# A graph network's second layer: its first pass in text order, and one square root for four blocks

## The chip, the core and the metric

The kernel runs on one core of one Trainium2 chip. The metric is the time of one launch on the device, in microseconds; lower is better. A core has five instruction queues: PE (matrix multiply), DVE (vector), ACT (scalar functions), POOL and SP. Each has an order of its own, and semaphores tie them together. SP only issues transfers here.

## The reference

32768 nodes with 128 features each, and 524288 edges. Two layers follow one another. The first is a graph layer with local attention and three batch norms. Its end matters here: the rows `x` plus a batch-normed `v` are layer-normed.

```python
# end of layer 0
x = _layernorm(x + _bn(h + f, g3, beta3))
# layer 1, three times
q = x @ Wq.T + bq
attn = softmax(q @ keys.T)
retrieved = attn @ values
lap = x - dinv[:, None] * segment_sum of (dinv[:, None] * x)[col] into row
x = 0.5 * x + 0.5 * (retrieved - 0.2 * lap)
# then a layer norm, the residual and a last layer norm
```

The stage under study works out the layer norm at the end of layer 0 for all rows, and the first of the three rounds of layer 1: the attention over 512 keys, and the rows scaled by `dinv`, which are spread out to the edges. Summing over the edges comes in the next stage.

## The kernel before

Nodes are handled in 64 blocks of 512 rows; a block has four chunks of 128 rows. `layer1_grid` has three stages, each with its own pools: the first pass (pool `l1p`), two passes of `for t in range(T_STEPS - 1)` (pool `l1w`), and a last one. The change is in the first pass. It and `l1w` are not under `tc.manual_schedule()`: their instructions are ordered by the framework's scheduler, which takes them from the text by priority and readiness. The last stage is. Under `tc.manual_schedule()` each engine gets its instructions in the order in which the text issues them.

A block of the first pass goes through three lists of steps; each step has a place, a number from 0 to 23.

- `first` (lines 1968 to 1990): `load` brings `v` (L1973) and `x` (L1975) in on SP. `scale` (place 7) applies the batch norm to `v` on ACT (L1978). `turn` (12) transposes it on PE (four matmuls, L1984) and adds `x` on DVE (L1985). `norm` (15) is a layer norm: four pairs of bn_stats and bn_aggr on DVE (L1080, L1081), a square root on ACT (L1083), a reciprocal (L1087) and four normalizing steps on DVE (L1089); then the rows are stored (L1989).
- `prepare` (1992 to 2017): `rows` (1) scales the rows by `dinv` (`nx`, L1998); four split steps (4, 8, 10, 14) cut them into three bf16 parts, alternating ACT (L1395, L1397) and DVE (L1396, L1393), and store them (L1394). `project` (2) transposes the rows (L2005, copy `xT` on ACT, L2007), `query` (7) multiplies by `Wq` (L2011, L2013).
- `emit` (2019 to 2070): `scores(c)` for the four chunks (0, 3, 6, 9) is a 512-column matmul (L2028), the row maximum on DVE (L1060) and the exponential on ACT with its sum (L1062). `turn(c)` (5, 8, 11, 13) transposes the probabilities (L2034) and copies them as `pt` on ACT (L2035). `retrieve` (17) sums four 512-column matmuls with `values` (L2040), copies the result as `oT` on ACT (L2043) and inverts the sums on DVE. `remain` (20) transposes it back (L2052) and makes `part_o` in two DVE steps (L2054, L2055), stored by L2056. `spread(n)` at every place from 0 to 23 is two matmuls with 384 columns (a pair, L1444) into a PSUM tile `exp`, of which there are two, and one eviction to bf16 (L1449): on ACT for even n, on DVE for odd n. Three evictions fill a tile that SP stores (L1452). `ask_pick` fetches the selection matrix of a chunk two chunks ahead (L1407).

`placed` merges the lists by place. In iteration n the loop issues `load` of block n+3, `first` of block n+2, `prepare` of n+1 and `emit` of n.

```python
return [f for _, f in sorted((x for one in lists for x in one), key=lambda x: x[0])]
```

PSUM has two tiles each of `exp`, `s` (scores, query, retrieve) and `tr` (all transposes). A pair can start only when the eviction that frees its tile is done.

Of the kernel before, what the change touches and what calls it, by code (L numbers as in the profile page):

```python
# [9 lines left out]
F32 = mybir.dt.float32  # L10
# [3 lines left out]
AF = mybir.ActivationFunctionType  # L14
OP = mybir.AluOpType
# [4 lines left out]
P = 128  # L20
D = 128
BLK = 512
NCH = BLK // P
# [885 lines left out]
def tile_gnn_resnorm(ctx: ExitStack, tc: tile.TileContext, a: dict, out: bass.AP):  # L909
# [8 lines left out]
    nc = tc.nc  # L918
    N = a["x"].shape[0]
    E = a["src"].shape[0]  # L920
    NB = N // BLK
# [38 lines left out]
    eps_c = cp.tile([P, 1], F32, name="eps_c")  # L960
# [9 lines left out]
    v = {n: vec[:, k:k + 1] for k, n in enumerate(VECS)}  # L970
# [125 lines left out]
    def layer_norm(wp, y, o, scale=None, shift=None):  # L1096
        for f in layer_norm_steps(wp, y, o, scale, shift):
            f()
# [856 lines left out]
    def layer1_grid(v_d, s3, c3):  # L1955

        exs = [Exchange("src", slots_d[t % 2], rows_d[t]) for t in range(T_STEPS)]
        with tc.tile_pool(name="l1g", bufs=1) as gp:
# [6 lines left out]
                if w < NW:  # L1965
                    picked[w] = exs[0].known_pick(wp, w)

            def first(b, st, wp, p_tr):


                def load():
                    st["v"] = wp.tile([P, BLK], F32, name="vT")
                    nc.sync.dma_start(st["v"], v_d[b])  # L1973
                    st["x0"] = wp.tile([P, NCH, D], F32, name="x1")
                    nc.sync.dma_start(st["x0"], rows_of(a["x"], b))  # L1975

                def scale():
                    nc.scalar.activation(st["v"], st["v"], AF.Identity, bias=c3, scale=s3)  # L1978

                def turn():  # L1980
                    st["x"] = wp.tile([P, NCH, D], F32, name="xn", bufs=5)
                    ps = p_tr.tile([P, NCH, P], F32, name="tr")
                    for c in range(NCH):
                        nc.tensor.transpose(ps[:, c, :], st["v"][:, c * P:(c + 1) * P], ident)  # L1984
                    nc.vector.tensor_add(st["x0"], st["x0"], ps)  # L1985

                def norm():
                    layer_norm(wp, st["x0"], st["x"])
                    nc.sync.dma_start(kept_of(xs_d[0], b), flat(st["x"]))  # L1989
                return load, [(7, scale), (12, turn), (15, norm)]  # L1990

            def prepare(t, b, st, wp, p_s, p_tr):

                ex = exs[t]

                def rows():
                    nx = wp.tile([P, NCH, D], F32, name="nx")
                    nc.vector.tensor_tensor(nx, st["x"], dinv[:, b * NCH:(b + 1) * NCH].unsqueeze(2)  # L1998
                                            .to_broadcast([P, NCH, D]), OP.mult)
                    st["r"], st["split"] = ex.split_steps(wp, b, nx, nx)  # L2000

                def project():
                    ps = p_tr.tile([P, NCH, P], F32, name="tr")
                    for c in range(NCH):
                        nc.tensor.transpose(ps[:, c, :], st["x"][:, c, :], ident)  # L2005
                    st["xT"] = wp.tile([P, BLK], F32, name="xT")
                    nc.scalar.copy(st["xT"], ps.rearrange("p c n -> p (c n)"))  # L2007

                def query():
                    ps = p_s.tile([P, BLK], F32, name="s")  # L2010
                    nc.tensor.matmul(ps, w["WqT"], st["xT"], start=True, stop=True)  # L2011
                    st["q"] = wp.tile([P, BLK], F32, name="qT")
                    nc.scalar.activation(st["q"], ps, AF.Identity, bias=v["L1_gnn_bq"])  # L2013
                return [(1, rows), (2, project), (4, lambda: st["split"][0]()), (7, query),
                        (8, lambda: st["split"][1]()), (10, lambda: st["split"][2]()),
                        (14, lambda: st["split"][3]())]

            def emit(t, b, st, wp, p_e, p_s, p_tr, share):

                ex = exs[t]  # L2020
                y = {}

                def scores(c):
                    if c == 0:
                        st["pt"] = wp.tile([P, NCH, BLK], F32, name="pt")
                        st["sums"] = wp.tile([P, NCH], F32, name="sums")
                    s = p_s.tile([P, BLK], F32, name="s")
                    nc.tensor.matmul(s, st["q"][:, c * P:(c + 1) * P], keysT, start=True, stop=True)  # L2028
                    st["pr", c] = softmax_rows(wp, s, st["sums"][:, c:c + 1])

                def turn(c):
                    ps = p_tr.tile([P, NCH, P], F32, name="tr")
                    for k in range(NCH):
                        nc.tensor.transpose(ps[:, k, :], st["pr", c][:, k * P:(k + 1) * P], ident)  # L2034
                    nc.scalar.copy(st["pt"][:, :, c * P:(c + 1) * P], ps)  # L2035

                def retrieve():
                    ps = p_s.tile([P, BLK], F32, name="s")
                    for k in range(NCH):
                        nc.tensor.matmul(ps, values[:, k, :], st["pt"][:, k, :], start=(k == 0),  # L2040
                                         stop=(k == NCH - 1))
                    st["oT"] = wp.tile([P, BLK], F32, name="oT", bufs=1)
                    nc.scalar.copy(st["oT"], ps)  # L2043
                    rec = wp.tile([P, NCH], F32, name="rec")
                    nc.vector.reciprocal(rec, st["sums"])
                    nc.vector.tensor_scalar(rec, rec, 0.5, None, op0=OP.mult)
                    st["rec"] = rec

                def remain():
                    ps = p_tr.tile([P, NCH, P], F32, name="tr")  # L2050
                    for c in range(NCH):
                        nc.tensor.transpose(ps[:, c, :], st["oT"][:, c * P:(c + 1) * P], ident)  # L2052
                    part = wp.tile([P, NCH, D], F32, name="part_o")
                    nc.vector.tensor_tensor(part, ps, st["rec"].unsqueeze(2).to_broadcast([P, NCH, D]), OP.mult)  # L2054
                    nc.vector.scalar_tensor_tensor(part, st["x"], 0.4, part, op0=OP.mult, op1=OP.add)  # L2055
                    nc.sync.dma_start(kept_of(part_d, b), flat(part))  # L2056

                def spread(n):
                    c, m = divmod(n, KS)
                    i = b * NCH + c  # L2060
                    if m == 0:
                        ask_pick(wp, i + 2)
                    ex.spread(wp, p_e, "exp", i, picked[i], st["r"][:, c, :], m, y, n % share == share - 1)
                    if m == KS - 1:
                        del picked[i]

                places = [(n, lambda n=n: spread(n)) for n in range(NCH * KS)]
                return places + [(0, lambda: scores(0)), (3, lambda: scores(1)), (5, lambda: turn(0)),
                                 (6, lambda: scores(2)), (8, lambda: turn(1)), (9, lambda: scores(3)),
                                 (11, lambda: turn(2)), (13, lambda: turn(3)), (17, retrieve), (20, remain)]  # L2070

            def placed(*lists):

                return [f for _, f in sorted((x for one in lists for x in one), key=lambda x: x[0])]
# [54 lines left out]
            def run(steps):  # L2129
                for f in steps:  # L2130
                    f()

            with tc.tile_pool(name="l1p", bufs=2) as wp, \
                    tc.tile_pool(name="l1p_exp", bufs=2, space=PSUM) as p_e, \
                    tc.tile_pool(name="l1p_s", bufs=2, space=PSUM) as p_s, \
                    tc.tile_pool(name="l1p_tr", bufs=2, space=PSUM) as p_tr:
                sts, firsts = {}, {}
                for w0 in range(2):
                    ask_pick(wp, w0)
                for n in range(-3, NB):  # L2140
                    b = n + 3
                    if b < NB:
                        sts[b] = {}
                        load, firsts[b] = first(b, sts[b], wp, p_tr)
                        load()
                    lists = []
                    if n + 2 in sts:
                        lists.append(firsts.pop(n + 2))
                    if n + 1 in sts:
                        lists.append(prepare(0, n + 1, sts[n + 1], wp, p_s, p_tr))  # L2150
                    if n >= 0:
                        lists.append(emit(0, n, sts[n], wp, p_e, p_s, p_tr, 2))
                    run(placed(*lists))
                    sts.pop(n, None)

            with tc.tile_pool(name="l1w", bufs=2) as wp, \
                    tc.tile_pool(name="l1_seg", bufs=2, space=PSUM) as p_g, \
# [3 lines left out]
                for t in range(T_STEPS - 1):  # L2161
                    sums = Sums(exs[t], wp, p_g, gc["iota1"], 2)
                    sts = {}
# [3 lines left out]
                    for n in range(-2, NB):  # L2167
                        lists = []
# [107 lines left out]
```

## Time and profile before

| | |
|---|---|
| median of three runs | 13724.5 us (13710.27 to 13725.8) |
| the profiled execution, its time | 13720.72 us |
| its span | 13718.8 us |
| PE, DVE, ACT, POOL busy over the whole span | 85%, 74%, 49%, 39% |
| first pair of the first pass starts | 6259.7 us |
| last eviction of the first pass ends | 7709.0 us |
| stage after it (`l1w`) | to about 12030 us |

How to read the lines of the profile: PE is the matmul queue, PEld its weight loads. A group names the line, the engine, the operation, what it writes and reads with the shapes, and the count; then its busy time and the mean of one instruction, and the time for which the engine stood idle just ahead of such instructions, with what ended most of it. L12 is line 12 of the kernel. A matmul of f32 operands shows as two records. In the timeline the first number is the start in the span, the second the time to the end of the row's instructions, and brackets hold the idle time before it with its releaser. A matmul's end is modelled, and one instruction's span overlaps the next one's start a little, so the time from start to start is shorter than the span.

### The profile page before, as it was taken

Reading aid. Unit: us, or ns where it says so; the run is one execution under the profiler, and the core shown is the slowest. Engines: PE = TensorE matmul, PEld = TensorE weight load, DVE = VectorE, ACT = ScalarE, POOL = GpSimd, SP = SyncE. Lnnn points to the kernel's source line nnn. Section 1 sums busy time; section 2 is a strip of 40 time slices with the busy share of each in tenths; the row PEclk is TensorE's granted clock in tenths of the full one; section 3 lists DMA queues with packets and bytes.
Section 4 is the critical chain, followed back from the end, with each engine's and each line's share of the span. In section 5 each row is a group of like instructions: output and inputs, shape, how many; then the busy total and the mean of one; then the engine's idle time right before and its main releaser. Section 6 shows DMA issues by size and latency. Waiting matters only on the chain. (4 is left out here: it accounts for less than half of the span.)

```text
span 13718.8 us, 167775 instructions
## 1 busy us (share of the span) xinstructions
PE 11728.4 (85%) x58924; PEld 5767.8 (42%) x58984; DVE 10087.5 (74%) x16572; ACT 6762.4 (49%) x10444; POOL 5314.5 (39%) x5333
## 2 busy tenths in 40 slices
PE   8988898887777888888999799999899999966666
PEld 3333333333333444444444455555455555533333
DVE  6998898879997777767888666666566666566666
ACT  4444444448884111137888566666566666600000
POOL 0000000000003777720000366666566666567777
PEclk9999999999999999999999999999999999988777
DMA  1000000007778999967888899999999999988887
GB/s 41 13 11 12 18 13 11 14 34 277 273 294 312 314 314 315 314 229 261 304 311 310 315 402 401 398 399 399 357 400 400 398 398 401 378 302 289 288 291 256
DMA packets 1339021, 3590.33 MB, mean 262 GB/s; under 512 B 197298, under 2 KB 579154, under 8 KB 1337010
## 3 DMA queue, kind: packets, MB, share of 16 engines
q1 hardware_dynamic: 968816, 2936.78, 56.6%
q0 software_dynamic: 252608, 520.41, 11.9%
q10 hardware_dynamic: 116738, 122.29, 2.6%
q8 instruction: 465, 7.62, 0.2%
q14 instruction: 394, 3.23, 0.1%
HBM read 2075.81 MB, written 1502.97 MB: 261 GB/s over the span
## 5 line engine op out<-in xcount | busy, mean ns | idle before, releaser
L1462 POOL DMA_INDIRECT listed<-rows,other x5120 | 5169.1, 1010 | 4103.9 <-issue 3140.6
L1449 ACT CAST y_o<-exp 128x768 bf16<-128x768 f32 x4352 | 3317.6, 807 | 984.7 <-PE exp L1444 732.6
L1444 PE MATMUL exp<-rows,pick 128*128 128x384 bf16 x12288 | 2818.7, 329 | 414.7 <-ACT y_o L1449 247.9
L1487 PEld LDWEIGHTS <-oh 128*128 128x128 bf16 x19456 | 1982.9, 102 | 2664.4 <-issue 1608.4
L1487 PE MATMUL seg<-y_i,oh 128*128 128x384 bf16 x12288 | 2643.7, 346 | 20.0 <-DMA y_i<-slots 18.7
L1449 DVE CAST y_o<-exp 128x768 bf16<-128x768 f32 x1792 | 1711.3, 955 | 688.9 <-PE exp L1444 576.7
L1444 PEld LDWEIGHTS <-pick 128*128 128x128 fp8e4 x12288 | 1203.3, 98 | 2054.3 <-issue 1371.6
L1487 PE MATMUL seg<-listed,oh 128*128 128x384 bf16 (+1 forms) x5120 | 1303.5, 335 | 885.5 <-DMA listed<-rows,other 848.3
L1390 POOL MEMSET rows<- 128x8 bf16 x64 | 6.8, 107 | 4022.2 <-DMA attn_d<-aT 2859.3
L1639 ACT ACTIVATE pT<-s 128x1024 f32<-128x1024 f32 x1024 | 1027.5, 1025 | 999.5 <-PE s L1614 859.7
L2103 DVE SCALAR_TENSOR_TENSOR part_i<-seg,dinv,part_i 128x128 f32<-128x128 f32 x1536 | 532.6, 347 | 1331.9 <-PE seg L1487 1320.8
L1619 DVE TENSOR_REDUCE mx<-s 128x2 f32<-128x1024 f32 x1024 | 1239.9, 1222 | 312.4 <-PE s L1614 308.4
L1614 PE MATMUL s<-k,q 32*128 32x512 f32 x4096 | 1196.7, 665 | 89.3 <-ACT pT L1639 82.0
L1635 PE MATMUL s<-ql,k 32*128 32x512 f32 x4096 | 1129.4, 646 | 63.8 <-DVE ql L1629 36.1
L1083 ACT ACTIVATE ln_rs<-ln_mv,eps_c 128x4 f32<-128x4 f32 x192 | 57.2, 298 | 1642.2 <-DVE ln_mv L1081 1641.5
L2028 PE MATMUL s<-keysT,qT 128*128 128x512 f32 x1536 | 796.0, 600 | 2.7 <-ACT pr L1062 1.7
L1432 DVE TENSOR_SCALAR_CACHE_REDUCE pick<-row_p,lane 128x512 fp8e4<-128x512 f32 x768 | 555.2, 748 | 260.2 <-PE row_p L1421 243.9
L2040 PE MATMUL s<-pt,values 128*128 128x512 f32 x1536 | 725.9, 595 | 10.7 <-ACT pt L2035 10.4
L1473 DVE TENSOR_TENSOR oh<-iota,slot 128x2432 bf16<-128x2432 bf16 x512 | 724.6, 1415 | 3.0 <-DMA slots<-y_o 3.0
L1473 DVE TENSOR_TENSOR oh<-ramp_p,slot 128x2432 bf16<-128x2432 bf16 x512 | 724.2, 1415 | 3.4 <-DMA slots<-y_o 3.4
L1487 PE MATMUL seg<-common,oh 128*128 128x384 bf16 (+1 forms) x2048 | 632.8, 351 | 69.1 <-DMA common<-rows,shared 68.6
L1421 PE MATMUL row_p<-row,ident_b 128*128 128x512 bf16 x1476 | 587.1, 398 | 95.7 <-DVE pick L1806 88.9
(404 smaller groups left out, 14138.6 us busy)
## 6 DMA issues: line engine op xcount, KB each, us to landing
slots<-y_o SPq DMA_DIRECT2D x2048, 576.0 KB
y_i<-slots SPq DMA_DIRECT2D x1024, 1152.0 KB
pick<-pick SPq DMA_DIRECT2D x1024, 192.0 KB
listed<-rows,other POOLq DMA_INDIRECT x5120
rows<-rows SPq DMA_DIRECT2D x192, 384.0 KB
part_d<-part_o SPq DMA_DIRECT2D x192, 256.0 KB
part_i<-part_d ACTq DMA_DIRECT2D x192, 256.0 KB
rows<-rows SPq DMA_DIRECT2D x64, 386.0 KB
```

What stands on the lines that cost most here:

```text
L1421: nc.tensor.matmul(ps, gc["ident"][:, w % P:w % P + 1].to_broadcast([P, P]), self.row[:, w // P, j * BLK:(j + 1) * BLK], start=True, stop= ...
L1444: nc.tensor.matmul(ps[:, j, :ROW], pick[:, o:o + P], r, start=True, stop=True)
L1449: (nc.vector.tensor_copy if to_dve else nc.scalar.copy)(dst, ps[:, :, :ROW])
L1462: nc.gpsimd.indirect_dma_start(out=g[:, k, :], out_offset=None, in_=self.table, in_offset=bass.IndirectOffsetOnAxis(ap=index[:, k:k + 1], ...
L1473: nc.vector.tensor_tensor(oh.rearrange("p c (w z) -> p c w z", z=2), ramp.rearrange("p (w z) -> p w z", z=2)[:, None].to_broadcast([P, NC2 ...
L1487: nc.tensor.matmul(ps[:, :n], oh[:, j, :], src, start=(k == 0), stop=(k == NC2 - 1))
L1614: nc.tensor.matmul(ps[:, s % 2, :], t["q", o][32 * s:32 * s + 32, c * P:(c + 1) * P], t["k", o][32 * s:32 * s + 32, :], start=True, stop=True)
L1619: nc.vector.tensor_reduce(m[:, c, 2 * i:2 * i + 2, xr[o]], st[b].pop(("two", i)), AX.X, OP.max, negate=True)
L1635: nc.tensor.matmul(ps[:, s % 2, :], t["k", o][32 * s:32 * s + 32, c * P:(c + 1) * P], t["ql", o][32 * s:32 * s + 32, :], start=True, stop= ...
L1639: nc.scalar.activation(t["p", c][:, 2 * i:2 * i + 2, :], ps, AF.Exp)
L2028: nc.tensor.matmul(s, st["q"][:, c * P:(c + 1) * P], keysT, start=True, stop=True)
L2040: nc.tensor.matmul(ps, values[:, k, :], st["pt"][:, k, :], start=(k == 0), stop=(k == NCH - 1))
```

## The change

The first pass is put under `tc.manual_schedule()`. The layer norm of `first` is cut in two. `moments` (place 15) takes the means and variances of a block into a tile that four blocks share; the last of the four takes one square root on ACT over all sixteen chunks (128x16 instead of 128x4) and one reciprocal on DVE. `norm` (place 14) is a list of its own and runs four blocks later. So the loop starts at -7 instead of -3: iteration n issues `load` of block n+7, `first` of n+6, `norm` of n+2, `prepare` of n+1 and `emit` of n. The tile of `v` has three buffers instead of two, that of `x` eight instead of two. `prepare` and `emit` are as before; below the change their line numbers are 20 higher.

```diff
--- before.py
+++ after.py
@@ -1965,29 +1965,49 @@
                 if w < NW:
                     picked[w] = exs[0].known_pick(wp, w)
 
-            def first(b, st, wp, p_tr):
-
+            def first(b, st, wp, p_tr, group):
+
+
+
+                k = b % NCH
 
                 def load():
-                    st["v"] = wp.tile([P, BLK], F32, name="vT")
+                    st["v"] = wp.tile([P, BLK], F32, name="vT", bufs=3)
                     nc.sync.dma_start(st["v"], v_d[b])
-                    st["x0"] = wp.tile([P, NCH, D], F32, name="x1")
+                    st["x0"] = wp.tile([P, NCH, D], F32, name="x1", bufs=2 * NCH)
                     nc.sync.dma_start(st["x0"], rows_of(a["x"], b))
 
                 def scale():
                     nc.scalar.activation(st["v"], st["v"], AF.Identity, bias=c3, scale=s3)
 
                 def turn():
-                    st["x"] = wp.tile([P, NCH, D], F32, name="xn", bufs=5)
                     ps = p_tr.tile([P, NCH, P], F32, name="tr")
                     for c in range(NCH):
                         nc.tensor.transpose(ps[:, c, :], st["v"][:, c * P:(c + 1) * P], ident)
                     nc.vector.tensor_add(st["x0"], st["x0"], ps)
 
+                def moments():
+                    if k == 0:
+                        group["mv"] = wp.tile([P, NCH, NCH, 2], F32, name="ln_mvs")
+                    st["mv"] = group["mv"]
+                    t = wp.tile([P, NCH, 6], F32, name="ln_st")
+                    for c in range(NCH):
+                        nc.vector.bn_stats(t[:, c, :], st["x0"][:, c, :])
+                        nc.vector.bn_aggr(st["mv"][:, k, c, :], t[:, c, :])
+                    if k == 0:
+                        group["rs"] = wp.tile([P, NCH, NCH], F32, name="ln_rss")
+                    st["rs"] = group["rs"]
+                    if k == NCH - 1:
+                        nc.scalar.activation(st["rs"], st["mv"][:, :, :, 1], AF.Sqrt, bias=eps_c)
+                        nc.vector.reciprocal(st["rs"], st["rs"])
+
                 def norm():
-                    layer_norm(wp, st["x0"], st["x"])
+                    st["x"] = wp.tile([P, NCH, D], F32, name="xn", bufs=5)
+                    for c in range(NCH):
+                        nc.vector.tensor_scalar(st["x"][:, c, :], st["x0"][:, c, :], st["mv"][:, k, c, 0:1],
+                                                st["rs"][:, k, c:c + 1], op0=OP.subtract, op1=OP.mult)
                     nc.sync.dma_start(kept_of(xs_d[0], b), flat(st["x"]))
-                return load, [(7, scale), (12, turn), (15, norm)]
+                return load, [(7, scale), (12, turn), (15, moments)], [(14, norm)]
 
             def prepare(t, b, st, wp, p_s, p_tr):
 
@@ -2134,24 +2154,27 @@
                     tc.tile_pool(name="l1p_exp", bufs=2, space=PSUM) as p_e, \
                     tc.tile_pool(name="l1p_s", bufs=2, space=PSUM) as p_s, \
                     tc.tile_pool(name="l1p_tr", bufs=2, space=PSUM) as p_tr:
-                sts, firsts = {}, {}
+                sts, firsts, norms, group = {}, {}, {}, {}
                 for w0 in range(2):
                     ask_pick(wp, w0)
-                for n in range(-3, NB):
-                    b = n + 3
-                    if b < NB:
-                        sts[b] = {}
-                        load, firsts[b] = first(b, sts[b], wp, p_tr)
-                        load()
-                    lists = []
-                    if n + 2 in sts:
-                        lists.append(firsts.pop(n + 2))
-                    if n + 1 in sts:
-                        lists.append(prepare(0, n + 1, sts[n + 1], wp, p_s, p_tr))
-                    if n >= 0:
-                        lists.append(emit(0, n, sts[n], wp, p_e, p_s, p_tr, 2))
-                    run(placed(*lists))
-                    sts.pop(n, None)
+                with tc.manual_schedule():
+                    for n in range(-NCH - 3, NB):
+                        b = n + NCH + 3
+                        if b < NB:
+                            sts[b] = {}
+                            load, firsts[b], norms[b] = first(b, sts[b], wp, p_tr, group)
+                            load()
+                        lists = []
+                        if n + NCH + 2 in firsts:
+                            lists.append(firsts.pop(n + NCH + 2))
+                        if n + 2 in norms:
+                            lists.append(norms.pop(n + 2))
+                        if 0 <= n + 1 < NB:
+                            lists.append(prepare(0, n + 1, sts[n + 1], wp, p_s, p_tr))
+                        if n >= 0:
+                            lists.append(emit(0, n, sts[n], wp, p_e, p_s, p_tr, 2))
+                        run(placed(*lists))
+                        sts.pop(n, None)
 
             with tc.tile_pool(name="l1w", bufs=2) as wp, \
                     tc.tile_pool(name="l1_seg", bufs=2, space=PSUM) as p_g, \
```

## The prediction

> **What bounds the kernel now.** The change touches one stage, the first pass of the second layer, so I read, in this order: the table of stages for its windows, the groups of ACT in it, the waits in it, and the timeline. The stage's first pair of spreading matmuls (L1444) starts at 6259.7 us and its last eviction (L1449) ends at 7709.0: 1449 us for 64 blocks, 22.6 us a block. The table of stages (length; busy time of PE, PEld, DVE, ACT, POOL; granted clock; DMA share; GB/s):
>
> ```profile
> 6900.00:7100.00 200.00, 180.53 (x838) 96.27 (x837) 174.43 (x332) 179.33 (x298) 0.00 (x0) 1.00 0.85 308
> 7100.00:7300.00 200.00, 180.61 (x843) 96.65 (x842) 175.45 (x325) 178.28 (x295) 0.00 (x0) 1.00 0.86 311
> ```
>
> Three engines are 87 to 90% busy at once. No one engine is the bound: the order keeps all three fed. DMA is not it: a later stage (7640 to 12000) moves 390 GB/s, this one 308. ACT's groups in the stage (count | busy us, mean ns | idle before):
>
> ```profile
> L1449 ACT CAST y_o<-exp 128x768 bf16<-128x768 f32 x726 | 582.8, 803 | 132.4 <-PE exp L1444 112.6 <-DMA slots<-y_o 5.0 <-issue 2.4
> L1062 ACT ACT_TABLE_LOAD x63 | 80.8, 1283 | 1.1
> L1083 ACT ACT_TABLE_LOAD x62 | 79.5, 1283 | 1.1
> ```
>
> ACT swaps its table twice a block. Waits (total us, times, longest):
>
> ```profile
> DVE y_o L1449 <- PE exp L1444: 120.3, 181, 1.7
> ACT y_o L1449 <- PE exp L1444: 112.6, 181, 2.5
> PE exp L1444 <- ACT y_o L1449: 53.4, 134, 0.9
> ```
>
> They are short: PE waits 78 us in all for the two PSUM buffers of "exp" (53.4 here, 24.5 for DVE). The timeline shows why. The four matmuls of "retrieve" (L2040, two records each) lie between pairs, so that evictions always have work:
>
> ```profile
> 6916.07 1.13 PE L2040 MATMUL s<-pt,values 128*128 128x512 f32 x2 [0.40 <-ACT pt L2035]
> ...
> 6917.03 0.81 PE L1444 MATMUL exp<-rows,pick 128*128 128x384 bf16 x4
> ...
> 6917.68 1.88 PE L2040 MATMUL s<-pt,values 128*128 128x512 f32 x4
> ...
> 6919.40 0.81 PE L1444 MATMUL exp<-rows,pick 128*128 128x384 bf16 x4
> ```
>
> At the end only spreading is left, and it runs at the pace of its buffers, 1.53 us per two evictions:
>
> ```profile
> 7697.17 0.96 DVE L1449 CAST y_o<-exp 128x768 bf16<-128x768 f32 x1 [0.57 <-PE exp L1444]
> 7697.49 0.80 ACT L1449 CAST y_o<-exp 128x768 bf16<-128x768 f32 x1 [0.79 <-PE exp L1444]
> 7698.18 0.81 PE L1444 MATMUL exp<-rows,pick 128*128 128x384 bf16 x4 [0.72 <-DVE y_o L1449]
> 7698.70 0.96 DVE L1449 CAST y_o<-exp 128x768 bf16<-128x768 f32 x1 [0.57 <-PE exp L1444]
> ```
>
> [...] The trace has 1283, and the square root starts 1.29 us after its load (7078.50 to 7079.79)[...], so I use 1.28. [...] a pair done at 7581.74 is cast at 7582.45, behind two exps queued ahead. So an engine's order is a chain of waits. [...]
>
> **The change, part by part.**
>
> *Square roots.* In the built kernels ACT's table loads go from 133 to 39: 94 x 1.283 = 121 us, 1.9 us a block. Square roots go from 64 to 16 (48 x 0.298 = 14 us), reciprocals from 64 to 16 on DVE (48 x 0.172 = 8 us). This is a gain only where ACT is late; below it isn't.
>
> *Order.* The built kernel's lists show each engine in text order, and retrieve's four matmuls run together. I walk one block with durations from the trace (in brackets the time until the engine can start its next): pair 0.49 (0.33); 512-column f32 matmul, one record after another, 1.02 (0.86); four transposes 0.60 (0.43); eviction on ACT 0.80 (0.69), on DVE 0.95 (0.87); exp with its sum (0.67); pt, oT, xT 0.59 (0.48); bf16 split 0.62 (0.52); v 0.83 (0.72); q 0.70 (0.60); DVE reduce or 512-wide add 0.69 (0.59 to 0.60), 0.73 where the next needs its result (7641.55 to 7642.28). A hand-over costs 0.04 us from PE and 0.06 to PE. Sn is the pair of step n, En its eviction (even on ACT, odd on DVE). The waits of the built kernel tell which eviction frees a pair's buffer: mostly two steps back, but S17 waits for E16, S18 for E15, S0 for E21, S6 for E5, S12 for E11. Start of each, us:
>
> - S17 0; retrieve 0.33, which holds PE 3.44; oT 3.97; E18 4.45; S20 5.31; transposes of oT 5.64; the two part_o steps 6.28, 7.01; E21 7.60; S0 of the next block 8.61.
> - Score 0 at 8.94; its max 10.00; nx 10.60; E1 11.19; S3 12.20; score 1 12.53; its max (behind E3) 13.60; exp 14.35; split 15.02; E4 15.54; pt 16.23; E6 16.71; exp of score 2 17.42.
> - v 18.09; q 18.81; E8 19.41; pt 20.10; exp of score 3 at 21.02 (its max waits behind E9, that for S9, E7, and the query matmul); split 21.69; E10 22.21; pt 22.90; E12 23.38; pt 24.07.
> - S14 24.24; E14 24.77; S16 25.63; E16 26.16; S17 of this block **27.02**.
>
> So 27.0 us a block, though DVE has some 19, PE 18.6 and ACT 17 us of work in it. In one block of four the square root sits between E14 and E16 and waits for DVE's moments, done at 27.74 (norm from 24.47, 1.04; the split's subtraction 0.59; four pairs of bn_stats and bn_aggr, each 0.39 since the second needs the first): E16 starts at 27.99, 1.83 late, with two evictions (E16, E18), oT and S17 behind it. The load back to exp costs 0.33 more (it ends at 11.11, exp could start at 10.75). (1.83 + 0.33) / 4 = 0.54. Sum: **27.56 us a block**.
>
> *DMAs.* They move with their steps on SP (loads of v and x ahead of each block, x_d, rows, part_d); a block has the same 6.6 MB over more time, and new buffers (3 for v, 8 for x, 2 groups) let loads run blocks ahead. I take 0; bounds 0 to +10 us. POOL has nothing in this stage.
>
> *Start and end.* Four blocks must be loaded and measured before the first norm: first pair some 5 us later (3 to 10), at 6264.5. Blocks at the end lack v and norm: about -5 us. The present tail of pure spreading (7662 to 7709, 47 us) goes away; that is inside the count.
>
> *Sum.* 6264.5 + 64 x 27.56 - 5 = 8023 against 7709: +315 us. The profiled execution took 13720.7 us (span 13718.8 and 1.9 around it), 3.8 below the median of 13724.5, so 13724.5 + 315 = **14040 us**, 2.3% slower. What is not in the trace is the coupling itself; bounds: each hand-over 0.02 more over some 35 hops is +45 us; a walk too strict by 1.5 us a block is -95.
>
> **Rivals.**
>
> - *Text order is too good: the saved table loads decide (faster).* ACT was busy 90%, the stage is full, and 1.9 us a block goes. If stalls stay small, DVE's 19.1 us bound it: 20.5 us a block ends at 7572, -137: 13590. It decides where a block takes under 22.6 us, that is, under 3.5 us of stall over DVE's work. Against it: retrieve alone holds PE for 3.44 us with only two buffers full.
> - *Strict rotation of the two buffers.* If S17 had to wait for E15, behind norm and moments, and S6 for E4, the same walk gives 30.6 us a block: +505, 14230. The built waits speak against it.
> - *Half the stalls.* If engines get ahead where I let them wait (score maxima, retrieve), 25 us a block: +150, 13875.
> - *The clock.* Gaps on PE could lower it: spreading at 72 to 74% busy had 0.92 to 0.96 (3400 to 4200 us). 6% of some 10 us of PE in the chain is 0.6 us a block, +38. My walk's longest PE gap is about 1.1 us, whereas the clock fell to 0.50 in the last stage after PE was busy 0.74 of 5 us (12625 to 12635). Taken as 0, kept in the range.
> - That the order isn't as the text says is excluded by the built lists.
>
> **How the numbers follow.** Forecast (13950 to 14130) 0.70; half the stalls 0.12; strict rotation 0.11; faster 0.05; within 0.2% 0.02. The range 13890 to 14170 leaves out the fast and equal cases and about half of two rivals. 0.2% (27 us) is about what a measurement of this kernel can tell from no change. Faster 0.05, same 0.02, slower 0.93.
>
> **What would show it.** In the profile after: the stage's windows at PE 65 to 70%, DVE and ACT 60 to 70%; 31 table loads in it; L2060 as one run of eight records per block, ahead of the longest waits of evictions for PE exp; large waits of exp (L1062) for the maxima (L1060) and of PE exp for evictions; a period near 27.5 us. Wrong, if the stage's period is under 22.6 us, or if PE's clock falls below 0.95 and makes the loss.

## The result, and the profile after

The changed kernel takes 14066.71 us (three runs, 14065.85 to 14076.24) against 13724.5: 1.0258 times as long, 95% interval 1.0244 to 1.0272. The forecast was 14040, the range 13890 to 14170.

The profiled execution after has a span of 14064.9 us, 346 more than before. The first pair starts at 6265.6 us and the last eviction ends at 8053.1: 1787.5 us for 64 blocks, 27.9 a block and not 22.6. That is 338 of the 346; 6 more come ahead of it, and the stage behind it takes as long as before within 5 us. The table of stages, in the windows shown of before:

```profile
6900.00:7100.00 200.00, 150.16 (x686) 80.77 (x685) 148.92 (x273) 130.78 (x226) 0.00 (x0) 1.00 0.71 255
7100.00:7300.00 200.00, 152.82 (x681) 81.57 (x681) 144.80 (x259) 126.86 (x218) 0.00 (x0) 0.99 0.69 250
```

PE is 76% busy, DVE 73%, ACT 64%: all three wait now. ACT's table loads in the stage have fallen from 125 to 31:

```profile
L1062 ACT ACT_TABLE_LOAD x16 | 20.5, 1283 | 0.3
L2001 ACT ACT_TABLE_LOAD x15 | 19.2, 1283 | 0.3
```

So the saving on ACT came, and the stage is longer all the same. The waits of the stage without its end, as before the change (total us, times, longest):

```profile
DVE y_o L1449 <- PE exp L1444: 315.6, 289, 5.1
ACT oT L2063 <- PE s L2060: 281.1, 63, 6.5
PE exp L1444 <- ACT y_o L1449: 265.6, 377, 2.8
...
ACT pr L1062 <- DVE nm L1060: 165.6, 193, 1.9
PE exp L1444 <- DVE y_o L1449: 150.6, 270, 1.2
```

PE waits 416 us for the two tiles of `exp` (78 before), and DVE waits for pairs 316 us (120 before). A new row stands second: ACT waits once a block for retrieve, 4.5 us on average. The timeline of PE shows two blocks, an ordinary one and one with the square root of four blocks:

```profile
7044.44 0.48 PE L1444 MATMUL exp<-rows,pick 128*128 128x384 bf16 x2 [0.89 <-ACT y_o L1449]
7044.76 3.60 PE L2060 MATMUL s<-pt,values 128*128 128x512 f32 x8
...
7100.26 0.48 PE L1444 MATMUL exp<-rows,pick 128*128 128x384 bf16 x2 [2.80 <-ACT y_o L1449]
7100.58 5.29 PE L2060 MATMUL s<-pt,values 128*128 128x512 f32 x8
```

The same eight records take 3.60 us in the first and 5.29 in the second, behind an idle time of 2.80. From 7100 to 7105 us the granted clock is 0.66 on average (0.50 for 3.41 us of it), from 7095 to 7100 it was 1.00.

### The profile page after: what moved, and what is told of

Read it like the earlier page. It is cut to its first block, busy times and chain, and to the rows that moved or that the text cites. A ratio compares the mean times of both kernels' runs of the same rounds, so it can differ in the third digit from the quotient of the medians.

```text
span 14064.9 us, 167947 instructions
## 1 busy us (share of the span) xinstructions
PE 11794.6 (84%) x58924; PEld 5801.3 (41%) x58984; DVE 10124.3 (72%) x16524; ACT 6629.1 (47%) x10302; POOL 5299.5 (38%) x5333
## 5 line engine op out<-in xcount | busy, mean ns | idle before, releaser
L1444 PE MATMUL exp<-rows,pick 128*128 128x384 bf16 x12288 | 2869.2, 330 | 740.2 <-ACT y_o L1449 461.8
```

The lines of the kernel that those rows point to most:

```text
L1444: nc.tensor.matmul(ps[:, j, :ROW], pick[:, o:o + P], r, start=True, stop=True)
```

## The experiments

The theory: the text order couples PE, ACT and DVE through two tiles of `exp`, and that makes the loss. The rivals: the grouped roots make it; or the clock; or DMA. All times are against the kernel before on the same chip: 13721 us for the first four, 13713 for the next four, 13717 for the last two. The changed kernel was timed beside one of 13724.5, so differences from its 14066.71 us hold to some 3 us in the first group and 11 in the second.

### Which half of the change

`e_roots` takes the hand-written order away and keeps the grouped roots:

```diff
-                with tc.manual_schedule():
-                    for n in range(-NCH - 3, NB):
+                for n in range(-NCH - 3, NB):
```

> Grouped square roots as in the changed kernel, but the first pass keeps the order that the scheduler gives it, as the kernel before has it. Theory (the text order makes the whole loss, by coupling the engines through the two PSUM buffers of exp): the loss is gone; ACT has 1.9 us a block less to do in a stage where three engines are 87 to 90% busy, so a block takes between 20.5 us (DVE's work and little stall) and the 22.6 us of before: 13590 to 13725 us, I take 13640. Rival (the grouped roots, their waits and the earlier loads bring a good part of the loss): slower than 13724.5.

Measured 13707.07 us, ratio 0.9989 (0.9982 to 0.9996). The loss is gone, but so is nearly all of the hoped gain. ACT's busy share falls to 82% between 6300 and 7500 us, and the last retrieve's transposes come at 7602.8 us, 59 earlier than before. The table of stages of `e_roots` shows where this goes:

```profile
7580.00:7600.00 20.00, 18.17 (x85) 9.53 (x84) 16.46 (x23) 15.35 (x27) 0.00 (x0) 1.00 0.77 290
7600.00:7620.00 20.00, 12.69 (x60) 5.77 (x59) 15.14 (x19) 11.93 (x17) 0.00 (x0) 1.00 0.84 321
...
7660.00:7680.00 20.00, 10.55 (x53) 4.98 (x52) 12.36 (x14) 10.39 (x13) 0.00 (x0) 1.00 0.86 321
```

From 7603 to 7695 the attention is done and the spreading is left, at the pace of its two buffers: 92 us of such a tail, against 47 before. The scheduler let the spreading fall behind the attention, and the tail gave back most of the 59 us.

`e_order` is the kernel before, its own norm in every block, with only the text order:

```diff
-                for n in range(-3, NB):
+                with tc.manual_schedule():
+                    for n in range(-3, NB):
```

> Text order alone: the first pass of the kernel before, each block with its own norm at place 15, put under the hand-written order. Theory: every block now bears what one in four bears in the changed kernel (a late square root 1.83 us, the load back to exp 0.33, a retrieve at a lower clock 1.69 us): 27.0 + 3.85 = 30.8 us a block against 22.6, so 13724.5 + 64 x 8.2 = 14250 us (14150 to 14400). Rival (the text order is harmless and the grouping makes the loss): within 30 us of 13724.5.

Measured 14130.49 us, ratio 1.0296 (1.0279 to 1.0313). So the order alone costs 409 us; the grouped roots then save 64, where in the scheduler's order they save 14. Some 26 of the 64 are fewer slow retrieves: 32 of 64 are slow here, 16 in the changed kernel. My size was 120 us too high, for two reasons that the trace shows. The normalizing steps come behind the root here, beside retrieve, so that the moments are done earlier and PE idles 1.81 us ahead of S17 and not 2.80. And only half of the retrieves are slow: for the most part blocks of 28.2 and 29.9 us alternate (mean 29.0), with 1.7 us between them. The idle time ahead is the same for both, as two blocks in a row show:

```profile
7147.68 0.48 PE L1444 MATMUL exp<-rows,pick 128*128 128x384 bf16 x2 [1.81 <-ACT y_o L1449]
7148.01 5.29 PE L2040 MATMUL s<-pt,values 128*128 128x512 f32 x8
...
7177.59 0.48 PE L1444 MATMUL exp<-rows,pick 128*128 128x384 bf16 x2 [1.81 <-ACT y_o L1449]
7177.91 3.60 PE L2040 MATMUL s<-pt,values 128*128 128x512 f32 x8
```

### Two parts of the stall by themselves

`e_split` spreads retrieve over four places:

```diff
-                    for k in range(NCH):
-                        nc.tensor.matmul(ps, values[:, k, :], ...)
+                    nc.tensor.matmul(ps, values[:, k, :], ...)
...
-                                 (11, lambda: turn(2)), (13, lambda: turn(3)), (17, retrieve), (20, remain)]
+                                 (11, lambda: turn(2)), (13, lambda: turn(3)), (23, remain)] + \
+                    [(17 + k, lambda k=k: retrieve(k)) for k in range(NCH)]
```

> The changed kernel with one edit: the four matmuls of retrieve come one each after the pairs S17, S18, S19 and S20, not four together after S17, and the transposes of its result come after S23, not after S20. Theory (retrieve holds PE for 3.44 us with only two buffers of exp full, so both evicting engines run dry): by the walk S0 of the next block comes some 1.7 to 2.5 us sooner, 64 x 2 = 130 us: 13940 us (13880 to 13990). Rival (retrieve's run lies beside other waits that then take its place, for instance exp waiting for the maxima): within 30 us of 14066.7.

Measured 14035.8 us (14017 to 14057), ratio 1.0223 (1.0206 to 1.024): 31 less than the changed kernel. The profiled execution is the slowest of the four, and its mean period is 28.2 us, no shorter at all. The rival comes nearest. My 1.7 to 2.5 us was a guess at one end of the chain; walked through to the next S17, the edit gives only 27.2 (an estimate made afterwards). The trace of `e_split` shows DVE's row between E13 and E15, then PE and ACT:

```profile
7036.50 1.11 DVE L2007 TENSOR_SCALAR xn<-x,ln_mvs,ln_rss 128x128 f32<-128x128 f32 x4
7037.52 0.68 DVE L1393 TENSOR_TENSOR rows<-nx,rows 128x512 bf16<-128x512 f32 x1
7038.13 0.28 DVE L1995 BATCH_NORM_STATS2 ln_st<-x 128x6 f32<-128x128 f32 x1
...
7039.73 1.79 DVE L1449 CAST y_o<-exp 128x768 bf16<-128x768 f32 x2
```

```profile
7039.58 1.91 PE L2061 MATMUL s<-pt,values 128*128 128x512 f32 x2
7041.28 0.84 PE L1444 MATMUL exp<-rows,pick 128*128 128x384 bf16 x2
```

E15 comes at 7039.73, behind 3.2 us of norm, split and moments, and S18 needs E15's tile (as the prediction's list has it): with the prediction's 0.95 us for E15 and 0.06 for the hand-over it cannot start before 7040.7 (an estimate), whatever retrieve does. Retrieve's long run had lain beside that row. PE's clock is lower too (0.94 in the stage, 0.98 in the changed kernel): this first matmul of retrieve takes 1.9 us and not 1.02 in nearly three of four blocks, which is most of the way from 27.2 to 28.2.

`e_root_late` puts the root where ACT waits for retrieve:

```diff
-                return load, [(7, scale), (12, turn), (15, moments)], [(14, norm)]
+                return load, [(7, scale), (12, turn), (15, moments), (16.5, root), (18.5, recip)], [(14, norm)]
```

> The changed kernel with one edit: the square root of four blocks is issued after E16 and its reciprocal after E18 and before E19, not behind the moments at place 15; so ACT does it, loads included, in the 4 us in which it waits for retrieve. Theory (in one block of four the late root costs 1.83 + 0.33 us and, by PE's idle 2.8 us ahead of S17, lowers PE's clock for a retrieve of 5.29 and not 3.60 us): every block takes 26.96 us and not 27.94 on average: -63, 14004 us, and every retrieve takes 3.6 us. Rival (the lower clock comes from PE's busy share in general): retrieves of 5.3 us remain, and only some 29 us come back, 14038 us.

Measured 14020.11 us, ratio 1.0219 (1.0202 to 1.0236): 47 less than the changed kernel. Blocks take 26.96 us, those with the root 27.28 (the load back to exp), so the late root is the 1.9 us. But 10 of the 64 retrieves still take 1.4 to 1.7 us more, and PE's idle time ahead of them is 0.89 us, as in nearly every other block. Both theories hold in part: without the long gap fewer retrieves are slow (10 and not 16), and a gap of 0.89 us can go ahead of a slow one too.

### Taking the stall apart

`e_dve` spreads DVE's row and leaves retrieve in one run. Its steps are the same, each with a place of its own (the diff gives places, not code):

```diff
-    norm: 14   last split step: 14   moments, root and reciprocal: 15
+    norm: 12, 13, 14, 15   last split step: 20   moments: 16, 17, 18, 19   root: 22   reciprocal: 23
```

> The changed kernel with DVE's row ahead of E15 taken apart: the four operations of norm at places 12 to 15, the four pairs of moments at 16 to 19, the last step of the split at 20, the square root at 22 and its reciprocal at 23; retrieve stays in one run. Theory (the stall of one place takes the place of another's: E15 waits behind 3.2 us of norm, split and moments on DVE while retrieve holds PE, so taking away one of the two alone gives little): the same walk gives 26.3 us a block against 27.94: 13962 us (13930 to 14070, the upper end if the two buffers go strictly in turn). Rival (DVE's row is the bound by itself): under 25 us a block, under 13880.

Measured 13960.49 us, ratio 1.0181 (1.0165 to 1.0196); the period is 26.15, with one of 26.86 in four, mean 26.3. The root has moved with the row; in `e_root_late`, where it alone moved, the period without slow retrieves is 27.0, so the rest of the row is worth 0.7 us a block. All 64 retrieves take 3.60 us here: the 247 us of loss that are left are not the clock's.

`e_both` adds the spread retrieve:

```diff
-    retrieve: 17 (four matmuls)   transposes of oT, part_o: 20
+    retrieve: 17, 18, 19, 20      transposes of oT, part_o: 22
```

> As the kernel with DVE's row taken apart, and retrieve's four matmuls also one each after S17 to S20, its transposes after S22. Theory (the two stalls cover each other): 24.8 us a block, 13868 us (13830 to 13960); that is 2.7 to 3.1 us a block against 0.5 (measured, retrieve alone) and 1.6 (expected, DVE's row alone). Rival (each is worth what it is worth alone): 13930 us or more.

Measured 13872.08 us, ratio 1.0116 (1.0101 to 1.0132); mean period 24.9. The spread retrieve, worth nothing to the period by itself, is worth 88 us once DVE's row is gone. By the walk it should give 0.7 us a block alone, and it gives 1.4 here: the two stalls covered each other. The clock has a part in it: in `e_split` it fell in 45 of 64 blocks, here in none.

`e_three` also issues each exp one place after its maximum:

```diff
-    exp of score 0 to 3: 0, 3, 6, 9
+    exp of score 0 to 3: 1, 4, 7, 10
```

> As the kernel with both edits, and each exp issued one place after its maximum, behind an eviction of ACT and not ahead of it. Theory (ACT waits for a maximum that DVE makes, with evictions queued behind): 23.6 us a block, 13789 us (13750 to 13870). Rival (exp's wait is covered by other waits): within 30 us of the kernel with both edits.

Measured 13797.2 us, ratio 1.0059 (1.0043 to 1.0074); mean period 23.7. ACT's wait for maxima falls from 149 us in `e_both` to 49 here (6300 to 7600 us). After these edits of the order (the later root among them) 84 us are left of a loss of 342.

### An order found by the walk

For `e_best` a small program repeated the walk over many orders and kept the shortest period. The operations are those of the changed kernel, except that two of the 24 evictions of a block go from DVE to ACT (places again):

```diff
+    scale -0.5  v transposed, added 1.5   moments 12, 15.5, 16.5, 19   root 19.5   reciprocal 23
+    norm 4.5, 15.5, 20, 23.9   nx 11.5   project 4.5   query 15   split 16.5, 19, 20, 23
+    scores, in the order 1, 3, 0, 2: matmul -0.5, 2, 6.5, 8   max 1, 3, 7.5, 8   exp 1, 3, 7.5, 9.5
+    turns, in the order 1, 3, 0, 2: transposes 4.5, 10, 10.5, 12.5   pt 6, 11.5, 12.5, 14.5
+    retrieve 16.5, 18, 19, 21   oT 21.5   remain 23   part_o 23.9
+    on DVE: evictions 2, 4, 5, 8, 10, 11, 14, 15, 19, 20; tiles exp0 and exp1 in turn
```

> The changed kernel with another text order: every operation of the stage at a place of its own, found by repeating the walk of the prediction over many orders, the score's matmul, maximum and exp apart, 10 of 24 evictions on DVE and not 12, and the two buffers of exp named so that they alternate. The same instructions otherwise. Theory (nothing but the order makes the loss; a text order can also be better than the scheduler's): 20.05 us a block against 22.6 before, 13724.5 - 64 x 2.55 = 13561 us (13540 to 13650). Rival (the stage has a bound at 22.2 us a block that no order passes, DMA or the clock, since the scheduler's order with the grouped roots did not get below it): 13700 us or more.

Measured 13613.27 us, ratio 0.9925 (0.9912 to 0.9939): faster than before, in text order. It took 52 us more than the walk gives. The next two ran on a chip on which the kernel before took 14830 us, so that only ratios and periods within a stage are read from them.

> The kernel in the order found by the walk once more, for its profile: 13613 us as measured, 1.0 us a block above the walk's 20.05. Theory (the walk has every wait but those for DMA): the stage takes 20.8 to 21.1 us a block and the difference shows as waits for a DMA. Rival (hand-overs and PE's clock take it): no waits for a DMA, and retrieves longer than 3.6 us in sum or a granted clock under 1.00 in the stage.

The walk knows no DMA; the trace of this order has waits for one. In `e_best_view`, a single run, from 6600 to 7800 us:

```profile
ACT y_o L1449 <- DMA slots<-y_o: 38.0, 46, 2.6
```

The stage takes 20.9 us a block. `e_best_3y` gives the evicted rows a third buffer in this stage:

```diff
-                st["y"] = wp.tile([P, 2, KS, ROW], BF16, name="y_o")
+                st["y"] = wp.tile([P, 2, KS, ROW], BF16, name="y_o", bufs=3 if tag in ("exp0", "exp1") else 2)
```

> The same order with three buffers and not two for the evicted rows (y_o) in this stage. Theory (the walk's missing 1.0 us a block is waiting for the writes of y_o to let its two buffers go): 20.2 us a block, 13613 - 50 = 13563 us (13550 to 13590). Rival (something else takes it): 13613 us within 15.

Measured on that chip: ratio 0.9891 (0.9874 to 0.9907). The wait is gone, and the period is 19.95, with one of 20.98 in four, mean 20.2. On another chip:

> The order found by the walk, with three buffers for y_o, on another chip. The profile of its first run shows 20.2 us a block (walk: 20.05) and no wait for y_o's writes, that of the kernel with two buffers 20.9 and 38 us of such waits. Theory: 13613 - 45 = 13568 us (13550 to 13590), 1.1% under the kernel before, as on the first chip. Rival: what it gained there was that chip's; within 15 us of 13613.

Measured 13567.05 us, ratio 0.9888 (0.9873 to 0.9903), the best version here. Its table of stages:

```profile
6900.00:7100.00 200.00, 196.61 (x930) 105.97 (x928) 183.16 (x341) 187.59 (x324) 0.00 (x0) 1.00 0.94 346
7100.00:7300.00 200.00, 196.41 (x929) 105.93 (x928) 182.34 (x340) 188.58 (x326) 0.00 (x0) 1.00 0.94 343
```

PE is 98% busy at full clock, and the order fits retrieve in between pairs:

```profile
7012.91 1.02 PE L2157 MATMUL s<-pt,values 128*128 128x512 f32 x2
7013.77 0.49 PE L1444 MATMUL exp<-rows,pick 128*128 128x384 bf16 x2
7014.09 1.02 PE L2157 MATMUL s<-pt,values 128*128 128x512 f32 x2
```

(These three lines are of `e_best_3y`.) Last, what the grouped roots are worth in this order. `e_best_each` takes one per block, with a reciprocal of its own:

```diff
-                    if k == NCH - 1:
-                        nc.scalar.activation(st["rs"], st["mv"][:, :, :, 1], AF.Sqrt, bias=eps_c)
+                    nc.scalar.activation(st["rs"][:, k, :], st["mv"][:, k, :, 1], AF.Sqrt, bias=eps_c)
```

> The same order and buffers, but each block takes its own square root and reciprocal at the places of the group's. ACT gets the 94 table loads back, 1.9 us a block. Theory (with the loads at a place where ACT has slack only the order counts): the walk gives 20.5 us a block against 20.05, +30 us: 13600 us (13580 to 13640). Rival (ACT is close to its bound in this order, 94% busy, so all of it shows): +120 us, 13690 us.

Measured 13627.02 us, ratio 0.9934 (0.9921 to 0.9948): 60 us more than `e_best_3y_again`, 30 above the walk's +30 and 60 below the rival's +120. Its period is 20.96 us and its ACT 99% busy:

```profile
6900.00:7100.00 200.00, 193.63 (x901) 102.41 (x899) 176.88 (x335) 198.84 (x337) 0.00 (x0) 1.00 0.91 333
```

Of ACT's 1.9 us a block 0.75 show in the period; PE goes from 98 to 97% busy and ACT from 94 to 99%, so the bound moves from PE to ACT.

## Why the prediction was right, and where its sum was off

- **The walk.** Right nearly to the hop in the block that I followed. From S17 at 7017.48 us, oT came after 3.96 us (3.97 predicted), E21 after 7.59 (7.60), the maximum of score 0 after 9.97 (10.00), the next S17 after 26.96 (27.02).
- **The root's block.** The square root came behind the moments, 0.99 us after its load had ended, and the period was 1.90 us longer (1.83 predicted), and 0.33 more for the load back.
- **The clock.** This is the term that was mis-sized. It was taken as 0 because "my walk's longest PE gap is about 1.1 us". That holds for three blocks in four. In the fourth S17 waits behind E16, and the walk's own figures give 0.9 + 1.83 = 2.7 us; the trace has 2.80. Of the 15 blocks with that gap 12 had a slow retrieve, and so had 4 of the other 49: 16 in all, 28 us, which is about the whole distance from 14040 to 14067. (Over the stage the clock is 0.98, above the 0.95 that I had named as a sign of being wrong.) `e_root_late` took the gap away and came out 47 us lower, not 63: its profiled execution, 20 us above the forecast, has 10 slow retrieves (15 us) and 15 loads back to exp (5 us).
- **The square roots.** 31 loads, as said. "A gain only where ACT is late" was the right question: the group is worth 14 us in the scheduler's order, 64 in this text order, 60 in the best one.
- **Start, end and DMA.** First pair at 6265.6 (6264.5 predicted). DMA was no wait worth naming at 27.9 us a block (2 us in the whole stage); it became one only at 20.9.
- **Busy shares.** PE's 76% and DVE's 73% lie above the 65 to 70 and 60 to 70 that I gave; the period does not rest on them.
- **Rivals.** Half the stalls and strict rotation both missed. "Text order is too good" was wrong for this order only: at 20.2 us a block `e_best_3y` passes the point from which that rival decides, 22.6.

What stays open: no run gave `exp` a third tile, so that its two tiles are what couples the engines rests on the waits (416 us) and on the walk, not on a run of its own. `e_best` changes more than the order, two evictions and the strict alternation of the tiles; what these are worth alone was not measured. And what lowers PE's clock in one retrieve and not in another was not shown, as the last section says.

## What to carry to other kernels

Before an order is fixed by hand, walk one period of every queue, with its buffers, and look for rows of work on one engine that another engine's tile waits behind; then walk the edit to the same point of the next period, since a stall that is removed alone may only uncover the one beside it. Work saved on an engine is worth what the order leaves exposed: here the same saving gave 14, 64 and 60 us. When the walk and the chip disagree, ask what the walk leaves out, here PE's clock and the buffers of a DMA.

## What had not been expected of the hardware

PE's clock fell in short stretches. The changed kernel's trace has 16 of them at 0.50 between 6300 and 8050 us: 13 last 3.41 us, three 6.83. Two windows of `e_root_late`, around a slow retrieve that starts at 7099.15 us:

```profile
7095.12:7098.54 3.42, 1.80 (x10) 0.82 (x9) 3.27 (x11) 2.73 (x4) 0.00 (x0) 1.00 0.82 283
7098.54:7101.95 3.41, 3.39 (x6) 1.65 (x6) 2.73 (x9) 0.00 (x0) 0.00 (x0) 0.50 0.79 312
```

PE was busy in 1.80 of the 3.42 us ahead of the fall. The gap did not decide alone: it is 0.89 us in 62 of the 64 blocks there, and 10 retrieves are slow; in `e_order` it is 1.81 us in 62 blocks, and 32 are slow. At 79% (`e_dve`) and 98% (`e_best_3y_again`) of the stage busy no retrieve was slow. What decides between a slow retrieve and another was not shown.
